# The MLP's second product in seven products of quarters instead of eight, in a two-layer convolution-and-attention kernel

## The chip, the cores and the metric

The kernel runs on one core of one Trainium2 chip. The metric is device time in microseconds (us), from the start of the program to its end. A core has five engines that run side by side[...]: PE (TensorE, matrix products; its weight loads are listed apart as PEld), DVE (VectorE), ACT (ScalarE), POOL (GpSimd) and SP (here only a queue of transfers). SBUF is the on-chip memory; PSUM is the small memory that TensorE writes its products to, in banks of 128 x 512 fp32.

## What is computed

All numbers are fp32. The input is x of 16 images, each 256 channels by 1024 positions. Layer 0 is an attention with 4 heads of 64; layer 1 is group norm, attention with 8 heads of 32, group norm and an MLP of 256, 1024 and 256 channels, each with a residual. Cut to what matters here:

```python
def layer1(x):
    x = x + attention(group_norm(x, gn1_w, gn1_b), qkv_w, proj_w, proj_b, phys_bias)
    h = group_norm(x, gn2_w, gn2_b)
    h = einsum('oc,bchw->bohw', mlp_w1, h) + mlp_b1      # 256 -> 1024
    h = gelu(h, approximate=False)
    h = einsum('oc,bchw->bohw', mlp_w2, h) + mlp_b2      # 1024 -> 256
    return x + h
```

The change concerns the second of the two MLP products, `mlp_w2` times the hidden activations.

## The kernel before

**Tiles.** Channels lie on the 128 partitions. 256 channels are two chunks (CC = 2), 1024 positions are two halves of TB = 512 (NT = 2) or eight blocks of 128 keys (SB = 8), and the 1024 hidden channels are HC = 8 chunks. An fp32 product is issued as two matmul instructions. `product` (L278) splits a product into column strips of width `cols[0]`: 32 during the attentions, 128 between them. So one 128x128 product is 8 matmul instructions during an attention and 2 outside.

**Order.** The order is written out by hand, and each engine takes its instructions in order. For each image b (L904):
1. `attention_a` (layer 0), 32 units of scores, exponentials and weighted sums. Its denominators are summed from the `es_a` tiles.
2. 16 `hidden` pieces (L806) of the *previous* image: product with w1 into PSUM, gelu by ACT into 16 tiles `g`. Between them the rest of layer 0's normalising, projecting and group norm is issued, by `Later.tick`, after so many steps.
3. Half of the layer-1 projections (L927).
4. `attention_b` (layer 1), 16 units, called u0 to u15 below: 4 items (a half of the positions and a chunk of heads), each with 4 steps kb = 0, 2, 4, 6. `fill` (L933 to L955) puts pieces of other work behind single units: the rest of this image's projections in u0 to u3, then the *previous* image's MLP outputs (`reduce`, L820; called o1 to o8) and the *next* image's layer-0 projections (P).

Before the change u4 to u15 hold, in the middle images: o1, o2, P, o3, o4, P, o5, o6, P, o7, o8, P, where a P is 2 or 3 pieces. Image 0 has neither outputs nor P there; the last image has o1 to o4 in u7, u9, u11 and u13, o5 to o8 after its attention, and its own MLP alone at the end.

**One unit of `attention_b`.** TensorE: scores of this unit (L470), the weighted sum of the unit before (L528), at the end of an item the denominator (L552), then the pieces. Scores use bank 0 and bank 1 and three `wide` tiles (L234) of PSUM. There are three `wide` tiles, taken in turn, least recently used first; a piece behind the unit takes the next one. ACT: four exponentials `e_b` (L485), a copy of the first weighted sum of an item. DVE: two adds of `e_b` into `es_b` (L507), the weighted sum added out of PSUM (L541, it frees bank 0 for the next unit), two more `es_b` adds, at some units `scale` (L577, the division by the denominator), and then the piece's own work. Four of the eight `e` tiles are used by a unit.

**Denominators.** `den_copy` (L315) copies the sums by ACT into tile `d`; a transfer spreads them, DVE takes reciprocals, POOL adds both into the range check's totals `dsum` and `isum` (L304, L305), and transfers spread the result into tile `full`, which `scale` reads. In image 0 (items 2 and 3) and the last image (item 3) the last step's `e_b` tiles are not added by DVE but summed by extra denominator matmuls (`spared` and `apart`, L491, L549).

**The output pieces.** For a half of positions t, a chunk of output channels co and a quarter of positions, `reduce` sums eight products of 256 columns and DVE adds bias and residual in one instruction:

```python
for hc in range(HC):
    product(ps, k["w2"][:, hc, co * P : (co + 1) * P],
            gs[t, hc][:, half * n : (half + 1) * n], start=(hc == 0), stop=(hc == HC - 1))
y = xb[:, co, t * TB + half * n : t * TB + (half + 1) * n]
nc.vector.scalar_tensor_tensor(y, ps, k["m2b"][:, co : co + 1], y, ALU.add, ALU.add)
```

**Start.** POOL issues three loads of `wp`, makes the identity `ident` and then issues eight loads of small vectors (L120). `turn` (L876) turns the bias rows `brow` by `ident`; ACT needs the result to empty the first projections. The weights w1 and w2 are loaded by SP (L149).

Of the kernel before, what the change touches and what calls it, by code (L numbers as in the profile page):

```python
# [14 lines left out]
P = 128  # L15
# [39 lines left out]
def kernel(  # L55
# [35 lines left out]
    brow = const.tile([3 * HEADS0 // 2, P], F32, name="brow")  # L91
    for t in (1, 0, 2):
        if t == 0:
            bp = b_proj.rearrange("(g i t d) -> t g i d", i=2, t=3, d=D0)
            for u in range(3):
                nc.scalar.dma_start(
                    brow[u * 2 : (u + 1) * 2].rearrange("g (i d) -> g i d", d=D0), bp[u]
                )
        for cc in range(CC):
            (nc.gpsimd if cc else nc.scalar).dma_start(  # L100
                wp[:, cc, t],
                w_proj[cc * P : (cc + 1) * P, :].rearrange(
                    "p (h t d) -> p t h d", t=3, d=D0
                )[:, t],
            )


# [3 lines left out]
    ident = const.tile([P, P], F32, name="ident")  # L111
    make_identity(nc, ident)
    mhalf = const.tile([P, CC], F32, name="mhalf")
    nc.gpsimd.memset(mhalf, -0.5)
    ones = const.tile([P, D0], F32, name="ones")
# [27 lines left out]
    w2 = load_mat(mlp_w2T, "w2")  # L143


    def load_rest():
# [5 lines left out]
    gind = const.tile([P, P // GSZ], F32, name="gind")  # L152
    nc.vector.tensor_reduce(
        gind, ident.rearrange("p (g j) -> p g j", j=GSZ), AX.X, ALU.add
    )
    gavg = const.tile([P, P // GSZ, GSZ], F32, name="gavg")
    nc.vector.tensor_scalar(
        gavg,
        gind.unsqueeze(2).to_broadcast([P, P // GSZ, GSZ]),
        1.0 / GSZ,  # L160
        None,
        ALU.mult,
    )
    gavg = gavg.rearrange("p g j -> p (g j)")
# [13 lines left out]
    with ExitStack() as first:  # L178
        first_pass(
            first, tc, x, out,  # L180
            dict(
                wp=wp, bqk=bqk, pb=pb, bo=bo, g1w=g1w, g1b=g1b, g2w=g2w,
                g2b=g2b, pjb=pjb, m1b=m1b, m2b=m2b, wo=wo, wq=wq, wpj=wpj, w1=w1,
                w2=w2, ident=ident, gavg=gavg, mhalf=mhalf, ones=ones, eones=eones,
                bvo=bvo, brow=brow, load_rest=load_rest, exp_bias=exp_bias,
                in_range=in_range,
            ),
        )

    good = nc.values_load(in_range[0:1, 0:1], min_val=0, max_val=1)  # L190
    with tc.If(good == 0):
        with ExitStack() as again:
# [5 lines left out]
                    w2=w2, ident=ident, gavg=gavg, mhalf=mhalf, b_proj=b_proj,  # L198
# [4 lines left out]
def first_pass(ctx, tc, x, out, k):  # L203
# [89 lines left out]
    def denominators(key, d, n, waits, then):  # L293
# [3 lines left out]
        full = work.tile([P, CC * TB], F32, tag="full", name=f"rd_{key}", bufs=1)[:, :n]  # L297
# [16 lines left out]

    def den_copy(key, den):  # L315
        d = work.tile([P, TB], F32, tag="d", name=f"d_{key}", bufs=1)
        nc.scalar.copy(d, den)
        return d
# [5 lines left out]
    def attention_a(b, qT, kT, v, project):  # L324
# [58 lines left out]
        def normalise(t):  # L383
            half = TB // 2
            den = wide(f"den_{key}_{t}")[:, 0, :]
            for c in range(CC):
                for g in range(2):
                    for h in range(2):
# [3 lines left out]
                            k["ones"][:, :32],  # L392
# [3 lines left out]
                        )  # L396
            denominators(
                f"{key}_{t}", den_copy(f"{key}_{t}", den), CC * TB,
# [47 lines left out]
    def attention_b(b, qT, kT, v, project):  # L446
# [44 lines left out]
        spared, apart = {0: (2, 3), B - 1: (3,)}.get(b, ()), {}  # L491

        def add(i, kb, es, block):
            if kb == 0 and block == 0:
# [4 lines left out]
                return  # L501
            if i in spared and kb == SB - 2:
                apart[i] = es
                return
# [40 lines left out]
        def normalise(i, r, last):  # L545
# [3 lines left out]
            parts = sums[i] + apart.get(i, [])  # L549
            for m in range(0, len(parts), G // 2):  # L550
                for g in range(G):
                    nc.tensor.matmul(  # L552
                        den[g * D : (g + 1) * D, :],
                        k["eones"][:, c * G + g],
                        parts[m + g // 2][:, g % 2, :],
                        start=(m == 0),
                        stop=(m + G // 2 == len(parts)),
                    )
            if at_end:

                full = work.tile([P, CC * TB], F32, tag="full", name="rd_end", bufs=1)
                nc.vector.reciprocal(full[:, :TB], den)
                scale(i, r, last, full[:, :TB])
                for tot, what in ((dsum, den), (isum, full[:, :TB])):
# [5 lines left out]
                f"{key}_{i}", den_copy(f"{key}_{i}", den), TB,  # L570
# [231 lines left out]

    def mlp(b, xb, hn):
        gs = {}

        def hidden(t, hc):  # L806
# [11 lines left out]
            gs[t, hc] = g  # L818

        def reduce(t, co, half):  # L820
            n = TB // 2
            ps = wide(f"m2_{b}_{t}_{co}_{half}")[:, 0, :n]
            for hc in range(HC):
                product(
                    ps,
                    k["w2"][:, hc, co * P : (co + 1) * P],
                    gs[t, hc][:, half * n : (half + 1) * n],
                    start=(hc == 0),
                    stop=(hc == HC - 1),
                )  # L830
            y = xb[:, co, t * TB + half * n : t * TB + (half + 1) * n]
            nc.vector.scalar_tensor_tensor(
                y, ps, k["m2b"][:, co : co + 1], y, ALU.add, ALU.add
            )

            each = b == B - 1 and (t, co) == (NT - 1, CC - 1)
            if half or each:
                sl = slice(t * TB + (half * n if each else 0), t * TB + (half + 1) * n)
                nc.sync.dma_start(out[b, co * P : (co + 1) * P, sl], xb[:, co, sl])
# [3 lines left out]
            [  # L843
                lambda t=t, co=co, half=half: reduce(t, co, half)
                for t in range(NT) for co in range(CC) for half in range(2)
            ],
# [23 lines left out]
    nothing = work.tile([P, TB], F32, tag="d", name="nothing", bufs=1)  # L870
    nc.vector.memset(nothing, 0.0)
    keep_warm(nothing, 3)
    xs = {0: load_x(0)}
    k["load_rest"]()
    ps, n = bank("bqk", 0), k["brow"].shape[0]
    turn = nc.tensor.transpose(ps[:, :n], k["brow"], k["ident"][:n, :n])  # L876
# [8 lines left out]
    k["exp_bias"]()  # L885

# [17 lines left out]
    for b in range(B):  # L904
# [32 lines left out]
        if b == B - 1:  # L937

            now, end = outputs[:4], outputs[4:]
        if not first:  # L940

            fill = {m: [piece] for m, piece in enumerate(own[:5:2] + own[1::2] + own[6:])}
            fill.update({len(own) + 2 * m: [piece] for m, piece in enumerate(now)})
# [4 lines left out]
        if first:  # L948
            fill[at - 1] = fill[at - 1] + first[:1]
            fill[last + 1] = first[-1:]  # L950
            pairs = [first[1:4], first[4:7], first[7:9], first[9:-1]]
            for m, pair in enumerate(pairs):
                rest.insert(3 * m + 2, pair)
# [20 lines left out]
    for j, (what, most) in enumerate(((dsum, DEN_MAX), (isum, 1.0 / DEN_MIN))):  # L974
        top = small.tile([P, 1], F32, tag="top", name=f"top_{j}")
        nc.vector.tensor_reduce(top, what, AX.X, ALU.add)
        nc.vector.tensor_scalar(ok[:, j : j + 1], top, most, None, ALU.is_le)
    both = small.tile([P, 1], F32, name="both", bufs=1)
    nc.vector.tensor_mul(both, ok[:, 0:1], ok[:, 1:2])
    row = bank("ok_row", 0)  # L980
    nc.tensor.transpose(row[0:1, :P], both, k["ident"])
    least = small.tile([P, 1], F32, name="least", bufs=1)
    nc.vector.tensor_reduce(least[0:1], row[0:1, :P], AX.X, ALU.min)
    nc.vector.tensor_copy(k["in_range"][0:1], least[0:1])


def general_pass(ctx, tc, x, out, k):
# [19 lines left out]
    )  # L1007
    pbs = small.tile([P, HEADS1], F32, name="pbs", bufs=1)
# [8 lines left out]
    def attention(key, H, D, qA, kA, vA, scale, bias, resT):  # L1017
        nb = H // qA.shape[1]
        per = P // D
        for t in range(NT):  # L1020
            tb = slice(t * TB, (t + 1) * TB)
            for h in range(H):
# [17 lines left out]
                for j in range(QT):  # L1040
                    nc.tensor.transpose(
                        row[0:1, j * P : (j + 1) * P], nm[:, j : j + 1], k["ident"]
# [133 lines left out]
    with tc.For_i(0, B, 1) as b:  # L1176
# [38 lines left out]
        for t in range(NT):  # L1215
# [14 lines left out]
            out_proj("gm2", k["w2"], HC, lambda kc: g[:, kc, :], k["m2b"], xb, t, None)  # L1230
# [40 lines left out]
```

## Time and profile before

| what | value |
|---|---|
| median of 3 runs | 3769.32 us (3769.05 to 3769.46) |
| the profiled execution, its own time | 3769.52 us |
| its span | 3767.7 us |
| granted TensorE clock | 1.00 throughout |
| DVE and ACT busy | 59% and 54% of the span |
| `hidden` matmuls, L809 | 1024 x 128x512, 452.8 us |
| emptying of output pieces, L832 | 128 x 128x256, mean 481 ns |
| `es_b` adds, L507 | 884 x 128x1024, mean 1219 ns |
| weighted sums added out of PSUM, L541 | 192 x 128x512, mean 682 ns |
| bias and residual out of PSUM, L617 | 128 x 128x512, mean 746 and 750 ns |
| POOL adds of 128x16, L304 and L305 | 190, median 220 ns |

A row of a group names line, engine, operation, what is written from what, the shape and the count; then busy time, mean duration of one, and the idle time before. A row of the timeline gives start, duration, engine, line, operation and, in brackets, how long its engine was idle before it and what ended that. TensorE's matmuls are pipelined, so the distance of two starts says more than a duration. PE's busy share of 100% is of this kind too.

### The profile page before, as it was taken

The page shows a single profiled execution, that of the slowest core. Times are in us where ns is not written, and L with a number is a line of the kernel's source. Part 1 is how long each engine was busy: PE and PEld are TensorE (multiplying, and loading weights), DVE is VectorE, ACT ScalarE, POOL GpSimd, SP SyncE. Part 2 cuts the span into 40 slices and gives each one's busy share as a digit, 9 for nine tenths or more (in the row PEclk, how much of TensorE's full clock was granted, in tenths as well). Part 3 has the DMA queues.
Part 4 walks back from the last instruction along what each step waited for, and adds up shares of the span by engine and source line. Part 5 has one row for each costly group of instructions (what it writes and reads, how often), then busy time and mean ns, then how long its engine had stood idle before and what let it go on. Part 6 is the DMA issues. An engine that isn't in the chain of part 4 may idle for free.

```text
span 3767.7 us, 87484 instructions
## 1 busy us (share of the span) xinstructions
PE 3755.1 (100%) x38692; PEld 1484.6 (39%) x38692; DVE 2217.2 (59%) x2753; ACT 2035.1 (54%) x2624; POOL 78.2 (2%) x245
## 2 busy tenths in 40 slices
PE   9999999999999999999999999999999999999999
PEld 4334343343433434334343333333333433333335
DVE  4664656646566565665656656565565655646572
ACT  4655546555465554555556455554555556555462
POOL 1000000000000000000000000000000000000000
PEclk9999999999999999999999999999999999999999
DMA  2000000000001000010000000010010100000000
GB/s 85 13 13 13 30 13 16 27 13 30 12 16 33 7 30 12 19 30 8 30 13 22 27 10 28 11 33 16 13 30 7 33 16 13 30 7 22 15 11 23
DMA packets 62352, 78.30 MB, mean 21 GB/s; under 512 B 34990, under 2 KB 36782, under 8 KB 61966
## 3 DMA queue, kind: packets, MB, share of 16 engines
q1 hardware_dynamic: 59820, 71.85, 6.4%
q8 instruction: 304, 4.98, 0.6%
q14 instruction: 82, 0.67, 0.1%
q10 hardware_dynamic: 1746, 0.40, 0.1%
q0 software_dynamic: 400, 0.41, 0.0%
HBM read 54.28 MB, written 17.56 MB: 19 GB/s over the span
## 4 chain that ended last, share of the span: by engine, by line
PE 97%; DVE 1%; issue 1%; ACT 1%; DMA 0%; SPq 0%; DVEq 0%; ACTq 0%
PE s_b L470 13%; PE acc_b L528 12%; PE m L809 12%; PE m L281 12%; PE s_a L338 12%; PE acc_a L359 11%; PE qk_b L281 6%; PE qk_a L281 6%; PE v_b L281 3%; PE o L281 3%; PE v_a L281 3%; PE j L281 3%; PE den_b L552 2%; PE den_a L390 1%; DVE es_a L371 0%
## 5 line engine op out<-in xcount | busy, mean ns | idle before, releaser
L485 ACT ACTIVATE e_b<-s_b 128x1024 f32<-128x1024 f32 (+1 forms) x1280 | 982.7, 864 | 469.8 <-PE s_b L470 469.7
L507 DVE TENSOR_TENSOR es_b<-es_b,e_b 128x1024 f32<-128x1024 f32 x756 | 885.4, 1219 | 339.4 <-ACT e_b L485 339.3
L346 ACT ACTIVATE e_a<-s_a 128x1024 f32<-128x1024 f32 x512 | 521.4, 1025 | 359.7 <-PE s_a L338 349.3
L470 PE MATMUL s_b<-q,k 32*64 32x512 f32 x8192 | 535.5, 601 | 3.1 <-DVE res_b L541 2.4
L338 PE MATMUL s_a<-q,k 64*64 64x512 f32 x4096 | 532.6, 593 | 1.1
L359 PE MATMUL acc_a<-e_a,v 64*64 64x512 f32 x4096 | 528.5, 589 | 0.0
L371 DVE TENSOR_TENSOR es_a<-es_a,e_a 128x1024 f32<-128x1024 f32 x384 | 469.1, 1222 | 85.8 <-ACT e_a L346 73.8
L528 PE MATMUL acc_b<-e_b,v 128*32 128x512 f32 x4096 | 492.1, 598 | 0.0
L281 PE MATMUL m<-g,w 128*32 128x256 f32 (+1 forms) x7616 | 464.3, 379 | 0.0
L809 PE MATMUL m<-gn_h,w 128*128 128x512 f32 x1024 | 452.8, 596 | 0.0
L817 ACT ACTIVATE g<-m,m1b 128x512 f32<-128x512 f32 x256 | 176.0, 687 | 355.9 <-PE m L809 355.9
L281 PEld LDWEIGHTS m<-g,w 128*32 128x32 f32 (+1 forms) x7616 | 277.5, 112 | 215.3 <-issue 41.3
L470 PEld LDWEIGHTS s_b<-q,k 32*64 32x64 f32 x8192 | 174.2, 130 | 287.4 <-issue 146.8
L809 PEld LDWEIGHTS m<-gn_h,w 128*128 128x128 f32 x1024 | 191.0, 190 | 235.5 <-issue 235.2
L359 PEld LDWEIGHTS acc_a<-e_a,v 64*64 64x64 f32 x4096 | 161.9, 133 | 277.5 <-issue 237.2
L338 PEld LDWEIGHTS s_a<-q,k 64*64 64x64 f32 x4096 | 152.6, 133 | 278.1 <-issue 211.7
L541 DVE TENSOR_TENSOR res_b<-res_b,acc_b 128x512 f32<-128x512 f32 x192 | 131.0, 682 | 200.5 <-PE acc_b L528 200.5
L528 PEld LDWEIGHTS acc_b<-e_b,v 128*32 128x32 f32 x4096 | 108.5, 109 | 351.6 <-ACT e_b L485 194.7
L281 PE MATMUL qk_b<-gn_g,wq 128*32 128x512 f32 (+1 forms) x1280 | 234.1, 592 | 0.0
L281 PE MATMUL qk_a<-x,wp 128*32 128x512 f32 (+1 forms) x1856 | 231.1, 592 | 0.5 <-ACT k L722 0.5
L743 DVE TENSOR_TENSOR v<-v_b,eones 128x512 f32<-128x512 f32 x64 | 43.9, 686 | 291.2 <-PE v_b L281 291.2
L507 DVE TENSOR_TENSOR es_b<-e_b,e_b 128x1024 f32<-128x1024 f32 x128 | 150.6, 1217 | 0.0
(124 smaller groups left out, 2087.5 us busy)
## 6 DMA issues: line engine op xcount, KB each, us to landing
rd_a<-row_a SPq DMA_DIRECT2D x64, 256.0 KB
rd_b<-row_b SPq DMA_DIRECT2D x252, 64.0 KB
out_dram<-x SPq DMA_DIRECT2D x63, 256.0 KB
x<-in_x_dram SPq DMA_DIRECT2D x30, 512.0 KB
w<-in_L_conv_mlp_w_dram SPq DMA_DIRECT2D x2, 1024.0 KB
x<-in_x_dram SPq DMA_DIRECT2D x4, 256.0 KB
sp_b<-d_b SPq DMA_DIRECT2D x63, 8.0 KB
row_b<-inv_b SPq DMA_DIRECT2D x63, 8.0 KB
```

The lines of the kernel that those rows point to most:

```text
L281: nc.tensor.matmul(o[sl], w[:, sl], r, **flags)
L338: nc.tensor.matmul(s[h : h + HALF, g, :], kT[g * D : (g + 1) * D, c, kb * P + h : kb * P + h + HALF], qT[g * D : (g + 1) * D, c, t * TB : ...
L346: nc.scalar.activation(e, s, AF.Exp, scale=float(D) ** -0.5)
L359: nc.tensor.matmul(accs[i][h][g * D : (g + 1) * D, :], v[h * HALF : (h + 1) * HALF, kb, c * 2 + g], e[h * HALF : (h + 1) * HALF, g, :], st ...
L371: nc.vector.tensor_add(sums[i], held[i] if kb == 1 else sums[i], e)
L470: nc.tensor.matmul(outs[g][h : h + HALF, :], kT[g * D : (g + 1) * D, c, k0 : k0 + HALF], qT[g * D : (g + 1) * D, c, t * TB : (t + 1) * TB] ...
L485: nc.scalar.activation(to, s, AF.Exp, scale=float(D) ** -0.5)
L507: ins = nc.vector.tensor_add(d, es[n] if kb == 0 else d, es[2 * block + n])
L528: nc.tensor.matmul(acc[g * D : (g + 1) * D, :], v[:, kb + m, c * G + g], es[2 * m + g // 2][:, g % 2, :], start=(m == 0), stop=(m == 1),)
L541: nc.vector.tensor_add(r, r, acc)
L809: nc.tensor.matmul(ps, k["w1"][:, cc, hc * P : (hc + 1) * P], hn[0][:, cc, t * TB : (t + 1) * TB], start=(cc == 0), stop=(cc == CC - 1),)
L817: nc.scalar.activation(g, ps, AF.Gelu, bias=k["m1b"][:, hc : hc + 1])
```

## The change

The second MLP product is seen as a 2 x 2 block product: the weights in quarters A (output chunk by half of the hidden channels), the activations in quarters B (half of the hidden channels by half of the positions). Strassen's scheme forms it from seven products instead of eight; five of them take a sum or difference of two quarters of A, and likewise of B.

- The weights' sums are made once, by POOL, after four loads of quarters.
- The activations' sums are made per image in place, in tiles `g`: four instructions of 128x512 per sum. POOL makes them, for the last image DVE. Two differences are issued among the `hidden` pieces (after the 13th and the 16th), a sum each after products 2, 3 and 4.
- An output piece (o1 to o7) is now one product of 4 chunks and 512 columns. DVE adds or subtracts it into one or two quarters of the output; the first five pieces have two, the last two have one.
- u4 to u15 of the middle images hold o1, P, o2, o3, P, o4, P, o5, P, o6, P, o7, each P two pieces. The last image has o1 to o3 in u7, u10 and u13, the other four after its attention.
- To make room in SBUF: `d` is dropped (`attention_b` copies into `full`, `attention_a` into the tile of `k1`); `brow`, `ident` and `gind` borrow a tile `e` at the start, and with them two of the three loads of `wp` and the identity are issued after the small vectors and the first x; `spared` and `apart` are gone. The range check at the end takes a matmul with `ones` in place of a transpose.

```diff
+    w2s = const.tile([P, 7, HID // P // 2, P], F32, name="w2s")
...
+    for n, q in ((2, (0, 0)), (3, (1, 1)), (4, (0, 1)), (1, (1, 0))):
+        weights.append((w2s[:, n], quarter(*q)))
+    def sum_quarters():
+        q11, q22 = w2s[:, 2], w2s[:, 3]
+        nc.gpsimd.tensor_sub(w2s[:, 5], w2s[:, 1], q11)
+        nc.gpsimd.tensor_add(w2s[:, 1], w2s[:, 1], q22)
+        nc.gpsimd.tensor_sub(w2s[:, 6], w2s[:, 4], q22)
+        nc.gpsimd.tensor_add(w2s[:, 4], w2s[:, 4], q11)
+        nc.gpsimd.tensor_add(w2s[:, 0], q11, q22)
...
-    def denominators(key, d, n, waits, then):
+    def denominators(key, den, d, full, waits, then):
+        nc.scalar.copy(d, den)
...
-            if i in spared and kb == SB - 2:
-                apart[i] = es
-                return
...
     def mlp(b, xb, hn):
+        n4 = HC // 2
         gs = {}
+        add_to = nc.gpsimd if b < B - 1 else nc.vector
...
-            gs[t, hc] = g
+            gs[hc // n4, t, hc % n4] = g
+            if (t, hc) == (1, n4):
+                combine((1, 0), (0, 0), False)
+            if (t, hc) == (1, HC - 1):
+                combine((0, 1), (1, 1), False)
+
+        def combine(to, what, plus):
+            for i in range(n4):
+                d = gs[(*to, i)]
+                ins = (add_to.tensor_add if plus else add_to.tensor_sub)(
+                    d, d, gs[(*what, i)]
+                )
+                tc.keep_in_program_order(ins)
+
+        products = [
+            (2, (0, 0), [(1, 0, True, True), (1, 1, False, False)], ((0, 0), (1, 1))),
+            (5, (1, 1), [(0, 1, True, True), (0, 0, False, False)], None),
+            (3, (0, 1), [(0, 1, True, False), (1, 1, True, True)], ((0, 1), (0, 0))),
+            (4, (1, 0), [(0, 0, True, True), (1, 0, True, False)], ((1, 0), (0, 0))),
+            (1, (0, 0), [(0, 0, True, False), (1, 1, True, False)], None),
+            (6, (0, 1), [(1, 1, True, False)], None),
+            (7, (1, 0), [(0, 0, True, False)], None),
+        ]
+        missing = {(0, 0): 4, (0, 1): 2, (1, 0): 2, (1, 1): 4}
+
+        def reduce(number, right, outs, then):
+            ps = wide(f"m2_{b}_{number}")[:, 0, :]
+            for i in range(n4):
+                product(
+                    ps, k["w2s"][:, number - 1, i], gs[(*right, i)],
+                    start=(i == 0), stop=(i == n4 - 1),
+                )
+            for co, t, plus, bias in outs:
+                missing[co, t] -= 1
+                num = 2 if b == B - 1 and number == 7 else 1
+                for u in range(num):
+                    n = TB // num
+                    sl = slice(t * TB + u * n, t * TB + (u + 1) * n)
+                    y, p = xb[:, co, sl], ps[:, u * n : (u + 1) * n]
+                    if bias:
+                        nc.vector.scalar_tensor_tensor(
+                            y, p, k["m2b"][:, co : co + 1], y, ALU.add, ALU.add
+                        )
+                    elif plus:
+                        nc.vector.tensor_add(y, y, p)
+                    else:
+                        nc.vector.tensor_sub(y, y, p)
+                    if not missing[co, t]:
+                        nc.sync.dma_start(out[b, co * P : (co + 1) * P, sl], y)
+            if then:
+                combine(*then, True)
...
     xs = {0: load_x(0)}
+    brow, ident = k["at_start"](
+        work.tile([P, 2, TB], F32, tag="e", name="borrowed", bufs=8)
+    )
     k["load_rest"]()
...
     k["exp_bias"]()
+    k["sum_quarters"]()
...
-            now, end = outputs[:4], outputs[4:]
+            now, end = outputs[:3], outputs[3:]
...
-            fill.update({len(own) + 2 * m: [piece] for m, piece in enumerate(now)})
+            fill.update({len(own) + 3 * m: [piece] for m, piece in enumerate(now)})
...
-            pairs = [first[1:4], first[4:7], first[7:9], first[9:-1]]
-            for m, pair in enumerate(pairs):
-                rest.insert(3 * m + 2, pair)
+            for m, at_most in enumerate((1, 4, 6, 8, 10)):
+                rest.insert(at_most, first[2 * m + 1 : 2 * m + 3])
```

In `products` each row is: number, which quarter of B, the outputs it is added to (co, t, plus or minus, with bias or not), and the sum made in place after it.

## The prediction

> **What bounds the kernel now.** I read the page's busy line and chain of waits first, then the timeline of one image's second attention by engine (PE, DVE, PEld), then POOL.
>
> ```profile
> PE 3755.1 (100%) x38692; PEld 1484.6 (39%) x38692; DVE 2217.2 (59%) x2753; ACT 2035.1 (54%) x2624; POOL 78.2 (2%) x245
> ...
> PE 97%; DVE 1%; issue 1%; ACT 1%; DMA 0%; SPq 0%; DVEq 0%; ACTq 0%
> ...
> L281 PE MATMUL m<-g,w 128*32 128x256 f32 (+1 forms) x7616 | 464.3, 379 | 0.0
> ```
>
> TensorE is never idle and is 97% of the chain; the product to be shortened is 464.3 us of it. So any TensorE time removed or lost counts in full. But a "busy" PE also hides short waits, as its timeline shows:
>
> ```profile
> 2732.64 3.64 PE L281 MATMUL m<-g,w 128*32 128x256 f32 x64
> 2736.20 2.40 PE L470 MATMUL s_b<-q,k 32*64 32x512 f32 x32
> 2738.53 1.92 PE L528 MATMUL acc_b<-e_b,v 128*32 128x512 f32 x16
> 2740.27 3.64 PE L281 MATMUL m<-g,w 128*32 128x256 f32 x64
> 2743.84 1.97 PE L470 MATMUL s_b<-q,k 32*64 32x512 f32 x32
> 2745.74 1.92 PE L528 MATMUL acc_b<-e_b,v 128*32 128x512 f32 x16
> ```
> ```profile
> 2734.11 2.35 DVE L507 TENSOR_TENSOR es_b<-es_b,e_b 128x1024 f32<-128x1024 f32 x2
> 2736.38 0.68 DVE L577 TENSOR_TENSOR res_b<-res_b,rd_b 128x512 f32<-128x512 f32 x1
> 2736.98 0.48 DVE L832 SCALAR_TENSOR_TENSOR x<-m,m2b,x 128x256 f32<-128x256 f32 x1
> ```
> ```profile
> 2737.51 0.21 PEld L470 LDWEIGHTS s_b<-q,k 32*64 32x64 f32 x8 [0.24 <-DVE x L832]
> ```
>
> An output piece takes 3.57 (2732.64 to 2736.20). The scores after it took 2.33 from start to start (2736.20 to 2738.53), the next ones 1.90 (2743.84 to 2745.74): 0.43 lost. The last line names why: the last eight loads of the scores wait for DVE's L832. Every unit takes three `wide` PSUM tiles and the piece at its end a fourth, so the last tile of the next unit's scores is the one that the output piece wrote, and DVE must have emptied it. Two more cases in the last image (scores at 3633.34 and 3658.49) took 1.99 and 2.22, with L832 ending 0.91 and 1.14 after their start; above it ended 1.26 after. Losses 0.09, 0.32, 0.43 for 0.91, 1.14, 1.26 are one line: **loss = (end of the emptying, after the start of the next scores) - 0.82 us.** In an undisturbed unit DVE starts 0.14 after the scores do (2743.97 against 2743.84) and needs 0.48: nothing is lost.
>
> ```profile
> 198.98 1.10 POOL L304 TENSOR_TENSOR dsum<-dsum,sp_b 128x16 f32<-128x16 f32 x1 [17.01 <-DMA sp_b<-d_b]
> ```
> ```profile
> 198.78 4.66 DVE L507 TENSOR_TENSOR es_b<-es_b,e_b 128x1024 f32<-128x1024 f32 x4 [2.01 <-ACT e_b L485]
> ```
>
> A POOL add of 16 columns has a median of 0.22 us; this one, issued inside a DVE add that runs from 198.78 to about 200.0, ended at 200.08. POOL waited for the running DVE add, then got in before DVE's next.
>
> **What the Trainium skill says.** GPSIMD Engine Reference, section 3.1: a two-input fp32 add of 2048 columns took 4497 ns. No row here has such a width. From that and the 0.22 us at 16 columns I estimate 0.22 + 496 x 2.1 ns = 1.25 us for 512 (proportionally it would be 1.12). SBUF — State Buffer, section Who interferes with whom: a DVE instruction with two SBUF inputs contends with a GpSimd one that reads SBUF, the second to issue waiting; one with at most one SBUF input, outside the 2-port modes, does not. The first half agrees with 1.10 against 0.22; no run here shows the second. So `es_b` adds (both inputs in SBUF) will collide with the new sums, and adds out of PSUM should not.
>
> **The change, part by part.** In us; u4 is unit 4 of the 16 in the second attention.
>
> *TensorE.* Seven pieces of 32 matmul instructions at 512 columns replace eight of 64 at 256. `qk_a` shows the new shape: 48 in 5.27, so 32 in 3.5, the same as now. One piece per image goes: -3.57 in images 1 to 14, and the two waits of 0.43 go (now o5 in u10 and o8 in u14, both behind a `scale`): -0.86. That is -4.43 per image, the whole gain. The image period is 233.0 (`hidden` pieces start at 2613.34 and 2846.34).
>
> *Emptying the products.* Five of seven products are now added twice, over 512 columns. From L617, a bias add is 0.75 and the next instruction starts 0.66 after it; from L541, an add out of PSUM is 0.68 with 0.60 to the next. Each pair ends 0.14 + 0.66 + 0.68 = 1.48 after the scores start: 1.48 - 0.82 = 0.66 lost. By place:
> - o1 in u4, o4 in u9: 0.66 each. o3 in u7: 0.14 + 0.60 + 0.75, 0.67.
> - o2 in u6, where `scale` is due: DVE ends its `es_b` adds 7.38 into the unit (2703.28 against 2695.90), `scale` takes 0.60, the unit 7.21; so it starts at 0.77, ends at 2.11: 1.29 lost.
> - o5 in u11: two plain adds, 0.60, and 0.18 more from the contention below.
> - o6 in u13: one add, ends at 0.82, nothing. o7 in u15 is followed by no scores.
> Sum 4.06. The other units, u5, u8, u10, u12 and u14, hold projection pieces, which ACT empties.
>
> *Sums on POOL, images 0 to 14.* Eight subtractions lie in the hidden stage, behind the `rstd_g` power in POOL's queue (2634.83, after 10 of 16 hidden pieces; the first sum is emitted after 13), where DVE has only one-input work: nothing. Twelve additions, four each after o1, o3 and o4, start with the next unit. Alternating with `es_b` adds at 1.25 they delay the adds of u5 by some 2.9, to 9.7 after its start, while the unit, stretched by 0.66, takes 7.87 and the next `es_b` start 2.24 into u6: no loss. In u8 two of four `es_b` adds are absent. In u10, with `scale`, DVE ends at 10.25, and u11 begins its adds 0.15 to 0.18 late: the 0.18 above. The summed inputs are wanted in u11, u13 and u15, over 30 us later. Queued behind them on POOL are only `dsum` and `isum`, which nothing waits for, until `rstd_h` in the next stage. Bounds: 0 if they never collide; 3 per image if POOL keeps the port for its four adds in a row.
>
> Images 1 to 14: 14 x (-4.43 + 4.06) = **-5.2**.
>
> *No more `apart`.* Image 0, items 2 and 3, and image 15, item 3, lose 16 denominator matmuls each (194.42 to 196.25, 1.83) and get four `es_b` adds (4 x 1.14) on DVE. There units without pieces run at DVE's pace, 5 us against TensorE's 3.64. For item 2, the result add that the next unit's bank 0 waits for comes some 1.1 later, most of which the missing 1.83 pays: -0.7. For item 3, -1.8. Image 0: **-2.5** (from -4 to +5, where all eight adds would count). Image 15: one piece less among its units (u7, u10, u13 instead of u7, u9, u11, u13), but pairs of adds at DVE's pace and sums beside them; at the end the 3.36 reciprocal sets the pace, some 0.5 earlier: **-0.5** (-3 to +4).
>
> *The tail.* Seven pieces of 3.45 instead of eight (128 matmuls from 3733.39 to 3761): -3.45. Image 15's 20 sums run on DVE at 0.60, beside pieces of 3.45. The last product is emptied in halves, +0.35: **-3.1**.
>
> *The start.* On POOL `wp` for q and v and the identity now stand behind eight small loads of 0.74: 5.9 later. q's weights then land about 13.5 instead of 7.6; TensorE can do k's four pieces until 14.2, if they come first: **+1.5** (0 to 4). SP issues four quarters instead of one `w2`; they are wanted 250 us later. The five weight sums make POOL wait for them, with `dsum` at 64 us behind. `full` taking over from `d`, and `k1` in the first attention, have their old readers gone a unit or a stage before; nothing.
>
> Sum: -5.2 - 2.5 - 0.5 - 3.1 + 1.5 = -9.8 on a span of 3767.7, with 1.8 around it (run 3769.5): **3759.7**; the median shown is 0.2 below that run, so **3759.5**.
>
> **Rivals.**
> *Faster: the tile is free in time.* If the loss line does not hold beyond 1.26, the 3.57 is kept. For: all four losses seen are 0.43 or less. Against: three points on one line, and the load that names L832. Without any new loss: 3769.3 - 14 x 4.43 - 4.6 = 3703; with half of it 3731.
> *Slower: the POOL sums hold up the emptying itself.* Place: after o1, o3 and o4 the first sum is released by the same last matmul as DVE's pair. If an add with one SBUF input also waits for POOL, each pair ends one sum later: 1.25 x 42 = +52, so 3812; two sums, 3864. It decides from 0.42 per place (17.5 / 42), which takes the time over 3777. For: a TENSOR_TENSOR is the operation that made POOL wait above. Against: the skill's exception.
> *The change doesn't do what it says*, for instance TensorE waiting for late sums: 30 us of room against 5 us of work excludes it.
>
> **How the numbers follow.** Forecast 0.56 (3744 to 3776: the bounds of contention, image 0 and the start), faster rival 0.22, slower one 0.22. The measurement cannot tell changes within 0.2%, 7.5 us. Half of the forecast, and somewhat more, lies below 3761.8, most of the rest within 7.5 of before: faster 0.57, same 0.21, slower 0.22. The range cuts a tenth off either side: 3718 to 3792.
>
> **What would show it.** Right: period 232.6; L281 m of 3320 matmuls; `s_b` after o1, o3, o4 and o5 taking about 2.56, after o2 3.2, with loads waiting for DVE at the output adds, some 50 us over the trace; POOL adds of 128x512 at 1.25. Wrong: `s_b` at 1.90 there (faster rival), or output adds starting 1 us or more after the scores (slower one); a period below 231 or above 234.

## The result, and the profile after

| | before | after |
|---|---|---|
| median of runs beside each other | 3769.73 | 3781.56 |
| span of the profiled execution | 3767.7 | 3780.4 |
| its mean granted TensorE clock | 1.000 | 0.998 |

The ratio is 1.0031, with a 95% interval of 1.002 to 1.0042: the change made the kernel slower by 0.31%, where a fall of 0.27% was forecast. The time lies inside the range given (3718 to 3792), on the other side of the time before. One of the four runs of experiment e6 below was slow (4792.31 us at a granted clock of 0.752, the others at 0.998 or 0.999), and e6's time is the median of the other three.

First the page of the changed kernel: busy time by engine, the shares of the chain that ended last by engine, and the groups that the change touches.

```profile
PE 3751.6 (99%) x34349; PEld 1329.2 (35%) x34349; DVE 2459.8 (65%) x2850; ACT 2036.6 (54%) x2624; POOL 565.4 (15%) x550
...
PE 90%; DVE 4%; issue 3%; DMA 1%; ACT 1%; SPq 0%; POOL 0%; DVEq 0%; ACTq 0%; POOLq 0%
...
L527 DVE TENSOR_TENSOR es_b<-es_b,e_b 128x1024 f32<-128x1024 f32 x768 | 961.5, 1300 | 258.2 <-ACT e_b L512 256.5
...
L497 PE MATMUL s_b<-q,k 32*64 32x512 f32 x8192 | 588.9, 603 | 14.9 <-DVE x L895 6.8
L855 POOL TENSOR_TENSOR g<-g,g 128x512 f32<-128x512 f32 x300 | 458.8, 1553 | 760.4 <-PE m L309 739.7
...
L309 PE MATMUL m<-g,w2s 128*32 128x512 f32 (+1 forms) x3320 | 404.2, 592 | 0.0
```

The product has shrunk from 464.3 to 404.2 us of TensorE, so 60 us were really saved. TensorE is still 99% busy, but its share of the chain has fallen from 97% to 90% and VectorE's has risen from 1% to 4%: TensorE now waits, and most of that waiting is booked as busy time of the scores (`s_b`, 588.9 in all).

The span was then cut at five points found in the timeline: the first scores of image 0, the first `hidden` piece of images 0 and 14, the first of image 15, and the end. "Stage of image 15" is everything between the last two of these pieces.

| part of the span | predicted | before | after | measured |
|---|---|---|---|---|
| start, to the first scores | +1.5 | 28.22 | 34.08 | +5.9 |
| image 0, to its `hidden` | -2.5 | 255.19 | 253.02 | -2.2 |
| images 1 to 14, period | -5.2 | 233.00 | 233.45 | +6.4 |
| stage of image 15 | -0.5 | 160.60 | 166.03 | +5.4 |
| tail | -3.1 | 61.82 | 58.95 | -2.9 |
| sum | -9.8 | | | +12.6 |

Three lines of the table failed: the middle images, the start and the stage of image 15. They are shown in this order, from the timeline of the changed kernel (columns: start in us, duration in us, engine, line, operation, tiles and shapes, count, and in brackets the idle time before it with what ended it). Middle images first, the product o3 in a middle image:

```profile
2717.08 3.62 PE L309 MATMUL m<-g,w2s 128*32 128x512 f32 x32
...
2717.94 3.44 DVE L527 TENSOR_TENSOR es_b<-es_b,e_b 128x1024 f32<-128x1024 f32 x2
...
2718.30 6.67 POOL L855 TENSOR_TENSOR g<-g,g 128x512 f32<-128x512 f32 x4 [12.92 <-PE m L309]
...
2720.63 1.95 PE L497 MATMUL s_b<-q,k 32*64 32x512 f32 x24
...
2721.30 0.68 DVE L893 TENSOR_TENSOR x<-x,m 128x512 f32<-128x512 f32 x1
...
2721.90 0.74 DVE L889 SCALAR_TENSOR_TENSOR x<-m,m2b,x 128x512 f32<-128x512 f32 x1
...
2722.78 1.09 PE L497 MATMUL s_b<-q,k 32*64 32x512 f32 x8 [0.21 <-DVE x L889]
2723.80 0.16 PEld L548 LDWEIGHTS acc_b<-e_b,v 128*32 128x32 f32 x8 [0.81 <-ACT e_b L512]
```

The last eight matmuls of the scores wait for L889, the second add of the product, as predicted. It ends at 2722.64, 2.01 after the scores' start, and from scores to sums it takes 3.17 instead of 1.90: 1.27 lost, where 0.67 was predicted. The reason is POOL's row: its sums start at 2718.30, while the product still runs, because its matmuls release the tiles `g` one after the other. So they meet the `es_b` adds of the *same* unit (3.44 instead of 2.35), and VectorE reaches the product's adds 0.5 later.

The five places account for the period: 0.75, 1.40, 1.27, 0.75 and 0.74 are lost after o1 to o5, 4.91 in all, and 233.00 - 4.43 + 4.91 = 233.48, against 233.45 measured.

The start:

```profile
8.25 1.53 POOL L93 DMA_DIRECT2D wp<-in_L_conv_w_proj_dram  x2
...
10.57 1.12 PE L309 MATMUL qk_a<-x,wp 128*128 128x512 f32 x2
...
15.12 12.12 PE L309 MATMUL qk_a<-x,wp 128*128 128x512 f32 x22 [3.43 <-DMA wp<-in_L_conv_w_proj_dram]
```

POOL issues `wp` for q and v at 8.25, behind eight small loads. TensorE has two pieces of k and half a piece of q to do and then stands for 3.43. That is not the whole cost. From 13.2 to 20.0 the clock granted to TensorE was 0.50. A view of that stretch shows it (PEclk, the third figure from the end, is the granted clock):

```profile
core 0: us, PE busy (x) PEld busy (x) DVE busy (x) ACT busy (x) POOL busy (x), PEclk, DMA share, GB/s
13.20:20.00 6.80, 4.88 (x6) 2.18 (x7) 0.00 (x0) 0.69 (x1) 0.00 (x0) 0.50 1.09 332
```

The 4.9 us of matmuls from 15.12 to 20.0 ran at that clock, so some 2.4 more were lost: with the wait, 5.8 of the 5.9.

The stage of image 15, where no projections lie beside the attention:

```profile
3641.07 6.93 POOL L855 TENSOR_TENSOR g<-g,g 128x512 f32<-128x512 f32 x4 [8.43 <-PE m L309]
...
3641.59 4.06 DVE L527 TENSOR_TENSOR es_b<-es_b,e_b 128x1024 f32<-128x1024 f32 x2
...
3643.40 1.95 PE L497 MATMUL s_b<-q,k 32*64 32x512 f32 x24
...
3646.23 0.67 DVE L895 TENSOR_TENSOR x<-x,m 128x512 f32<-128x512 f32 x1
...
3647.05 1.09 PE L497 MATMUL s_b<-q,k 32*64 32x512 f32 x8 [1.70 <-DVE x L895]
```

Here VectorE is busy back to back, so the two `es_b` adds that POOL stretches from 2.35 to 4.06 are passed on whole, and TensorE idles 1.70. A second wait, 1.81 at 3691.53, ends with the result add that frees bank 0, behind another stretched pair. Here too the clock counts. After each of the two waits it was 0.50 for 3.41 us. In e3, an experiment below that changes only the start, the stage has waits of 1.71 and 1.82 but no such spell. The same view of the stage, first of the changed kernel, then of e3:

```profile
3555.39:3721.42 166.03, 161.31 (x1236) 56.14 (x1233) 117.35 (x142) 83.29 (x113) 33.09 (x32) 0.98 0.05 14
```
```profile
3552.90:3716.14 163.24, 158.05 (x1236) 55.69 (x1233) 117.36 (x142) 83.30 (x113) 33.10 (x32) 1.00 0.05 14
```

So 2.8 of the 5.4 are the two spells, and 2.6 are left.

### The profile page after: what moved, and what is told of

Its sections match the earlier page's. It is cut to its first block, busy times and chain, and to the rows that moved or that the text cites. A ratio compares the mean times of both kernels' runs of the same rounds, so it can differ in the third digit from the quotient of the medians.

```text
span 3780.4 us, 79539 instructions
## 1 busy us (share of the span) xinstructions
PE 3751.6 (99%) x34349; PEld 1329.2 (35%) x34349; DVE 2459.8 (65%) x2850; ACT 2036.6 (54%) x2624; POOL 565.4 (15%) x550
## 4 chain that ended last, share of the span: by engine, by line
PE 90%; DVE 4%; issue 3%; DMA 1%; ACT 1%; SPq 0%; POOL 0%; DVEq 0%; ACTq 0%; POOLq 0%
PE s_b L497 12%; PE m L836 12%; PE s_a L363 12%; PE acc_b L548 11%; PE acc_a L384 11%; PE m L309 7%; PE qk_b L309 6%; PE qk_a L309 5%; PE v_b L309 3%; PE o L309 3%; PE v_a L309 3%; PE j L309 3%; DVE es_b L527 2%; PE den_b L570 1%; PE den_a L415 1%
## 5 line engine op out<-in xcount | busy, mean ns | idle before, releaser
L527 DVE TENSOR_TENSOR es_b<-es_b,e_b 128x1024 f32<-128x1024 f32 x768 | 961.5, 1300 | 258.2 <-ACT e_b L512 256.5
L497 PE MATMUL s_b<-q,k 32*64 32x512 f32 x8192 | 588.9, 603 | 14.9 <-DVE x L895 6.8
L855 POOL TENSOR_TENSOR g<-g,g 128x512 f32<-128x512 f32 x300 | 458.8, 1553 | 760.4 <-PE m L309 739.7
L309 PE MATMUL m<-g,w2s 128*32 128x512 f32 (+1 forms) x3320 | 404.2, 592 | 0.0
L309 PEld LDWEIGHTS m<-g,w2s 128*32 128x32 f32 (+1 forms) x3320 | 122.2, 112 | 261.5 <-issue 246.6
```

The costliest lines, as they stand in the source:

```text
L309: nc.tensor.matmul(o[sl], w[:, sl], r, **flags)
L497: nc.tensor.matmul(outs[g][h : h + HALF, :], kT[g * D : (g + 1) * D, c, k0 : k0 + HALF], qT[g * D : (g + 1) * D, c, t * TB : (t + 1) * TB] ...
L527: ins = nc.vector.tensor_add(d, es[n] if kb == 0 else d, es[2 * block + n])
L855: ins = (add_to.tensor_add if plus else add_to.tensor_sub)(d, d, gs[(*what, i)])
```

## The experiments

Theory A: a product's PSUM tile is emptied too late, because VectorE first ends the unit's `es_b` adds and then needs two adds of 512 columns; POOL's sums make that worse only where they meet `es_b`. Rival B: POOL's sums are the loss. Rival C: VectorE's load is. The kernel before, run beside them, had medians of 3769.6 to 3770.0. All edits are to the changed kernel.

**e1_single_add.** Each product is added into its first output only (the counts in `missing` are set to match).

```diff
-            for co, t, plus, bias in outs:
+            for co, t, plus, bias in outs[:1]:
```

> Leaves out the second of the two adds of each of the products o1 to o5 (five of twelve adds per image), so part of the output's sum is missing; products, POOL sums, loads and order stay. Theory A (TensorE waits because the product's PSUM tile is emptied by two adds of 512 columns, 1.4 to 2.1 us after the next scores start, and every us past 0.74 is lost): with one add the emptying ends at about 0.14 + 0.68 = 0.82, after o2 (behind the scale) at about 1.45. So the losses of 0.75, 1.40, 1.27, 0.74, 0.74 fall to about 0.1, 0.7, 0.6 (o3 keeps what the POOL sums do to the adds before it), 0.1, 0.1: from 4.9 to 1.6 per image, 14 x 3.3 = 46 us, some 4 more in image 15's adds: about 3732, period 230.2. Rival B (the POOL sums beside the adds are the loss): the sums are still there, so the time stays within 10 us of 3781. Rival C (VectorE's total load): five adds of 0.67 less per image is under 2% of VectorE's busy time; a change of under 10 us.

Measured: 3737.56, ratio to before 0.9911 (0.9896 to 0.9927), 44.0 below the changed kernel; period 230.39. The timeline of TensorE in this run, after o1, o2 and o3:

```profile
2667.01 2.03 PE L497 MATMUL s_b<-q,k 32*64 32x512 f32 x32
2668.97 1.92 PE L548 MATMUL acc_b<-e_b,v 128*32 128x512 f32 x16
...
2681.45 2.68 PE L497 MATMUL s_b<-q,k 32*64 32x512 f32 x32
2684.06 1.92 PE L548 MATMUL acc_b<-e_b,v 128*32 128x512 f32 x16
...
2689.34 2.48 PE L497 MATMUL s_b<-q,k 32*64 32x512 f32 x32
2691.76 1.92 PE L548 MATMUL acc_b<-e_b,v 128*32 128x512 f32 x16
```

From start to start 1.96, 2.61 and 2.42: losses of 0.06, 0.71 and 0.52, against 0.75, 1.40 and 1.27. After o4 the loss is 0.06, after o5 0.42 where 0.1 was expected; why is not known. POOL's sums are unchanged here and `es_b` still has a mean of 1298 ns, so B falls as the main cause: one add less behind the `es_b` adds is worth 43 us in the middle images. C is not yet excluded: the five adds left out are 3.35 us of VectorE per image, about as much as the period fell. It falls in e6, where VectorE has more to do and the kernel is faster.

**e2_no_sums.** The in-place sums are left out.

```diff
-            for i in range(n4):
+            for i in range(0):
                 d = gs[(*to, i)]
```

> Leaves out the twenty in-place sums of activations of each image (on POOL in images 0 to 14, on VectorE in image 15), so that products 2 to 7 get other inputs; everything else stays. Theory A: only what these sums do to the es_b adds beside them goes: 0.6 per image after o3 (loss 1.27 to about 0.67), 14 x 0.6 = 8 us; in image 15's stage the two waits of 1.70 and 1.81 shrink, 3 to 5 us; at the end nearly nothing. About 3768, period 232.8. Rival B (the sums are what makes the change slower): the losses after o1, o3 and o4 all fall to near nothing, period about 230, time about 3735 or less.

Measured: 3767.08, ratio 0.9992 (0.9983 to 1.0), 14.5 below the changed kernel. The period is 232.92, so the sums cost 0.53 in each of 14 images, 7.4 in all. All of it is at o3, where the loss falls from 1.27 to 0.75; the other four places lose what they lost with the sums. The stage of image 15 falls from 166.0 to 158.6, by 7.5: 4.7 when compared with e3's stage without half-clock spells (163.24), and 2.8 for the two spells, which are gone together with the waits. So the whole rise of image 15, and 2.0 more, goes with POOL's sums. They are a real cost, but not the main one.

**e3_start** and **e7_start.** In e3 the loads of `wp` for q and v go directly behind those for k. In e7 the eight small loads go behind them instead:

```diff
         t = const.tile([P, n], F32, name=name)
-        nc.gpsimd.dma_start(t, v.rearrange("(c p) -> p c", p=P))
+        vectors.append((t, v.rearrange("(c p) -> p c", p=P)))
...
         make_identity(nc, ident)
+        for v, src in vectors:
+            nc.gpsimd.dma_start(v, src)
```

> The loads of the first attention's projection weights for q and v are issued directly after those for k, ahead of the small vectors, the identity and the load of the first image, as in the kernel before; nothing else changes. Theory A (5.9 us at the start are POOL's late issue of wp for q, for which TensorE waits 3.4 with only k's pieces to do): the first scores start 4 to 6 us earlier, at 28 to 30, and the whole time falls by that: about 3776.5. Rival (the start is set by the identity and the transposed bias, or by the later loads): no change, or slower by up to 2 us, since the identity and the biases' loads now come later.

> Only the loads of the eight small vectors move, behind wp for q and v and the identity in POOL's queue; ScalarE's queue keeps the bias rows ahead of its wp loads for q and v, which e3 had put behind them (TensorE then waited 2.69 for those rows). Theory A (the start costs what POOL's late wp costs): q's weights come before k's pieces end, first scores at 28 to 29.5 instead of 34.1, time about 3776. Rival (loads share one bandwidth, so the start is set by bytes): first scores stay at 31 or later.

e3: 3779.14, ratio 1.0023 (1.0014 to 1.0032); first scores at 31.72, less than expected, because the bias rows now stood behind `wp` in ScalarE's queue. e7: 3774.63, ratio 1.0012 (1.0006 to 1.0019), 6.9 below the changed kernel; first scores at 27.74. Its timeline:

```profile
2.44 1.50 POOL L93 DMA_DIRECT2D wp<-in_L_conv_w_proj_dram  x2
```
```profile
10.09 10.81 PE L313 MATMUL qk_a<-x,wp 128*128 128x512 f32 x24
...
27.74 1.95 PE L367 MATMUL s_a<-q,k 64*64 64x512 f32 x16
```

With `wp` issued at 2.44 the 24 matmuls run through without a wait, and the granted clock is 1.00 up to the first scores. So the start's +5.9, the wait and the spell of half clock with it, came from the place in POOL's queue.

**e4_order.** Only the order of the pieces changes: a product that is added twice has a projection piece behind it in the same unit.

```diff
-            for m, at_most in enumerate((1, 4, 6, 8, 10)):
-                rest.insert(at_most, first[2 * m + 1 : 2 * m + 3])
+            p = first[1:-1]
+            rest = [
+                [now[0], p[0]], [p[1]], [now[1], p[2]], [now[2], p[3]],
+                [p[4]], [p[5]], [now[3], p[6]], [now[4], p[7]],
+                [p[8]], [now[5]], [p[9]], [now[6]],
+            ]
```

> Only the order of the pieces in images 1 to 14 changes: in units 4 to 15 each product that is added twice is followed by a projection piece in the same unit (3.5 us on TensorE), units with one projection piece stand where pairs stood; number of pieces, sums and adds are the same, nothing is left out. Theory A (the loss is the emptying ending too late for the next scores' tile): VectorE is through with the unit's es_b adds before the piece that follows the product ends, so both adds end before the next scores start; the losses of 0.75, 1.40, 1.27, 0.74 and 0.74 go to 0 to 0.2 each: about 4.4 x 14 = 60 us, time about 3720, period 229.1. Rival B (contention of POOL sums with es_b adds slows the stage): the sums still run beside es_b adds, so at most 10 us are gained. Rival C (VectorE's load in the stage): no change.

Measured: 3776.67, ratio 1.0015 (1.0008 to 1.0022), only 4.9 below the changed kernel: a miss by 55. (A projection piece is also half as long as I wrote, 1.8 us.) The timeline shows why. After o1 theory A holds:

```profile
2695.76 0.75 DVE L889 SCALAR_TENSOR_TENSOR x<-m,m2b,x 128x512 f32<-128x512 f32 x1 [1.33 <-PE m L309]
...
2696.43 0.68 DVE L895 TENSOR_TENSOR x<-x,m 128x512 f32<-128x512 f32 x1
...
2697.34 1.97 PE L497 MATMUL s_b<-q,k 32*64 32x512 f32 x32
...
2699.24 0.16 PEld L548 LDWEIGHTS acc_b<-e_b,v 128*32 128x32 f32 x8 [0.81 <-ACT e_b L512]
```

Both adds end before the scores start, and from start to start it takes 1.90: nothing lost. After o2 and o5 nothing is lost either. But o4, now in a unit with `es_b` adds and a `scale`, met POOL's sums:

```profile
2738.36 7.39 POOL L855 TENSOR_TENSOR g<-g,g 128x512 f32<-128x512 f32 x4 [2.89 <-PE m L309]
...
2738.68 4.27 DVE L527 TENSOR_TENSOR es_b<-es_b,e_b 128x1024 f32<-128x1024 f32 x2
...
2742.47 1.11 PE L497 MATMUL s_b<-q,k 32*64 32x512 f32 x16
...
2742.87 1.76 DVE L595 TENSOR_TENSOR res_b<-res_b,rd_b 128x512 f32<-128x512 f32 x1
...
2744.55 0.74 DVE L889 SCALAR_TENSOR_TENSOR x<-m,m2b,x 128x512 f32<-128x512 f32 x1
2745.21 0.67 DVE L893 TENSOR_TENSOR x<-x,m 128x512 f32<-128x512 f32 x1
...
2746.03 1.12 PE L497 MATMUL s_b<-q,k 32*64 32x512 f32 x16 [2.44 <-DVE x L893]
```

The `es_b` pair takes 1.92 longer and the `scale` 1.08 longer, so the emptying starts 3.0 late. With two pieces in the unit the product's tile is wanted one step earlier too, by the second half of the scores, which wait 2.44. In all, 2.70 are lost after o4, and after o3, in the same way, 1.08.

The mean period of 233.15 hides a second thing. In eight of the 14 middle images it is 232.37 to 232.40. In the other six it is 233.71 to 235.38, and in each of these, beside the wait after o4, the granted clock was 0.50 for 3.41 us (in one 6.83). The 20 runs of e4 agree: the fastest, 3768.73, had a mean clock of 0.998, the slowest, 3783.12, one of 0.993. So without these spells the order alone is worth 1.07 per image.

So either theory A is incomplete, with a second limit behind the first, or the shorter units are the trouble. The next three runs separate these.

**e5_order_no_sums.** The edits of e4 and e2 together.

> The order of e4 without the in-place sums of activations (all twenty per image left out, so products 2 to 7 get other inputs). In e4 the losses after o1, o2 and o5 went, but o4's unit lost 2.9 on the scores and 1.5 on the product after them, while four POOL sums of 7.39 in all ran beside es_b adds (2 in 4.27 instead of 2.35) and the scale (1.76 instead of 0.68). Theory A with contention as second limit: without the sums both go, period about 228.6 (233.0 less 4.43), so 14 x 4.2 = 58 us below the run without sums in the old order: about 3709. Rival D (e4's gain is eaten because units with half a projection piece, 5.5 us, are too short for VectorE's 4.66 of es_b adds): the waits stay without the sums, time within 15 of 3767.

Measured: 3706.84, ratio 0.983 (0.9815 to 0.9845), period 228.62. The scores' group of this run:

```profile
L497 PE MATMUL s_b<-q,k 32*64 32x512 f32 x8192 | 527.6, 601 | 3.9 <-DVE res_b L561 2.6
```

`s_b` has fallen from 588.9 to 527.6 us, and the period is that of before less the 4.43 of the prediction's first step (228.57). The short units do no harm, so rival D falls. It also accounts for e4: with 1.08 and 2.70 lost, 228.60 becomes 232.38, the period of e4's images at full clock.

**e8_dve_only** and **e6_order_dve.** The twelve sums after o1, o3 and o4 on VectorE, in the old order and in that of e4, for images 0 to 13.

```diff
+            eng = nc.vector if plus and b < B - 2 else add_to
             for i in range(n4):
                 d = gs[(*to, i)]
-                ins = (add_to.tensor_add if plus else add_to.tensor_sub)(
+                ins = (eng.tensor_add if plus else eng.tensor_sub)(
```

> The changed kernel's order, with the twelve additions on VectorE instead of POOL in images 0 to 13; nothing left out. Theory A: the losses after o1, o2, o4 and o5 stay (two adds still end 1.4 to 2.1 after the next scores start), o3's falls by 0.6; the four sums behind o1, o3 and o4 end 2.4 later than the pair, pushing the next unit's es_b adds by about 1.7, which may cost o2 up to 1 more: 3775 to 3795. Rival B (POOL contention is the loss): about 3735 or less.

> The order of e4, and the twelve additions after o1, o3 and o4 on VectorE instead of POOL in images 0 to 13 (0.60 each, behind the product's own adds in VectorE's program); nothing left out. Theory A with contention: VectorE stands idle 2.5 to 3.2 behind the adds of o1 and o3 in e4, so 2.4 of sums fit there, behind o4 they push the next es_b adds by about 1.5, which the product in that unit covers; waits for the output adds go; period 228.6 to 229.2, images 1 to 14 about 60 below the changed kernel: about 3722 (3715 to 3735). Rival C (VectorE's load is the limit): 7.2 us more on VectorE per image make it slower than e4: 3777 or more.

e8: 3773.67, ratio 1.0009 (1.0 to 1.0017), period 232.95: as good as without sums (232.92), a little better than expected. e6: 3714.62, ratio 0.985 (0.9832 to 0.9868), period 228.73, nothing left out. The timeline around o4 in e6:

```profile
2691.37 2.36 DVE L527 TENSOR_TENSOR es_b<-es_b,e_b 128x1024 f32<-128x1024 f32 x2
...
2693.64 0.69 DVE L595 TENSOR_TENSOR res_b<-res_b,rd_b 128x512 f32<-128x512 f32 x1
...
2694.25 0.75 DVE L890 SCALAR_TENSOR_TENSOR x<-m,m2b,x 128x512 f32<-128x512 f32 x1
2694.91 0.68 DVE L894 TENSOR_TENSOR x<-x,m 128x512 f32<-128x512 f32 x1
...
2695.17 1.97 PE L497 MATMUL s_b<-q,k 32*64 32x512 f32 x32
...
2695.50 2.49 DVE L856 TENSOR_TENSOR g<-g,g 128x512 f32<-128x512 f32 x4
```

The same chain is undisturbed, ends 0.42 after the scores start (2695.59), and the sums follow in 2.49, behind what TensorE waits for. So the engine with the larger load does the sums at almost no cost (228.73 against 228.62 without any), and the idle one was the costly place. Rival C falls: with the twelve sums VectorE is busy for 2499.2 us of the run, against 2468.8 in e4, and the kernel is faster; e8, with 2501.9, has the same work and still loses 4.4 per image at the five places.

Set side by side, the four periods tell it best:

| sums on | old order | order of e4 |
|---|---|---|
| POOL | 233.45 | 233.15 |
| VectorE | 232.95 | 228.73 |

Either change alone is worth 0.3 to 0.5 per image, both 4.72. At full clock the order alone would be worth 1.07, which leaves the picture as it is: each change removes one of two limits, and the gain comes when both are gone.

**e9_both.** The edits of e6 and e7.

> The order and the VectorE additions of e6 together with the loads of e7; nothing left out. Theory A: the parts are in different places of the trace and add up: 3715.2 of e6 less 7.0 (e7 against the changed kernel): about 3708 to 3711, 1.6% below the kernel before. Rival (what is gained at the start is lost again later, as waits that only the start's offset had hidden): 3715.

Measured: 3706.95, ratio 0.9835 (0.9822 to 0.9849): 1.65% faster than the kernel before, and nothing left out. That is 1 us below the range expected; counted from e6's 3714.6 the sum of the parts is 3707.7, so they add up. In its stage of image 15 (164.3), where the sums of image 14 are still on POOL, some 6 us are left by comparison with e5 (158.6), one spell of half clock among them; no run tried to get them.

## Why the prediction was wrong

Forecast and measurement are 22.4 us apart, from -9.8 to +12.6: 11.6 in the middle images, 5.9 in the stage of image 15, 4.4 at the start and 0.5 in the rest. The middle images alone, with their two terms, take the sum to +1.8; no single term would have turned the sign.

*TensorE, -4.43 per image:* right; e5 and e6 show it almost whole (periods of 228.62 and 228.73, against 233.00 before).

*Emptying the products:* the mechanism was right, and all five places lose as named: 0.75, 1.40, 1.27, 0.75 and 0.74, the same in all 14 images, against 0.66, 1.29, 0.67, 0.66 and 0.78. Two terms were mis-sized. The constant of the loss line, 0.82 from ends of 0.91 to 1.26, is 0.74 at ends of 1.48 to 2.14 (1.48 - 0.75, 2.14 - 1.40, 2.01 - 1.27): some 0.08 at each place. At o5 this is hidden, because 0.18 had been allowed for contention and the loss is 0.74 with the sums and without them (e2). So 0.3 per image is left, and no run explains it. The other term is o3, next.

*Sums on POOL:* the step that failed is "Twelve additions, four each after o1, o3 and o4, start with the next unit." At o1 and o3 they start inside the product, 1.2 us after its first matmul. At o3 they meet `es_b` adds that stand ahead of the emptying, and that cost 0.52 (1.27 against 0.75 without sums, e2), 7.3 over 14 images. At o1 the `es_b` adds beside them end in time, since VectorE then waits 1.33 for the product. At o4 they start with the next unit, as I had written, because `isum` stands ahead of them on POOL; there, as worked out, they were hidden. Together the two terms make +0.84 per image, 11.8 over 14 images, which turned -5.2 into +6.4 (measured by the period). The sum of the middle images was a small difference of two large terms, 4.43 and 4.06, so 20% of one was enough to change its sign.

*Image 15, -0.5 (-3 to +4):* this failed, at +5.4 it left even its bounds. "sums beside them" got no number of its own; they measured 4.7, since nothing hides them in a stage that runs at VectorE's pace, and the two spells of half clock after their waits 2.8 more. Without them the stage is 2.0 shorter than before (e2). Without the spells the rise would have been 2.6, inside the bounds.

*The start, +1.5:* failed. "TensorE can do k's four pieces until 14.2, if they come first" left the condition open: two come first, and the third piece is q's. TensorE waited 3.43, and the half clock beside the wait, for which the prediction has no term anywhere, cost some 2.4 more. The total was 5.9.

*Image 0 and the tail:* right, -2.2 and -2.9 against -2.5 and -3.1.

*The 1.25 us for a POOL add of 512 columns,* worked out from the GPSIMD Engine Reference, section 3.1: undisturbed ones took 1.26 and 1.27. (0.22 + 496 x 2.1 ns is in fact 1.26.) The mean of 1553 ns includes the waiting for VectorE.

*Rivals.* The faster one is excluded: the line keeps rising beyond 1.26, one us lost for each us later. The slower one had the sign but not the mechanism. The timeline of the changed kernel around o1, with POOL's sums running:

```profile
2694.59 4.73 POOL L855 TENSOR_TENSOR g<-g,g 128x512 f32<-128x512 f32 x3 [39.32 <-PE m L309]
...
2696.92 2.72 PE L497 MATMUL s_b<-q,k 32*64 32x512 f32 x32
2697.06 0.75 DVE L889 SCALAR_TENSOR_TENSOR x<-m,m2b,x 128x512 f32<-128x512 f32 x1 [1.33 <-PE m L309]
...
2697.72 0.68 DVE L895 TENSOR_TENSOR x<-x,m 128x512 f32<-128x512 f32 x1
```

The adds out of PSUM start 0.14 after the scores and take 0.75 and 0.68, as without POOL's sums (e2). That agrees with the Trainium skill (SBUF — State Buffer, Who interferes with whom): an add with one input in SBUF is not held up, one with two is. It is the adds *ahead* of the emptying in VectorE's queue, `es_b` and `scale`, that POOL delays.

## What to carry to other kernels

When a change makes one engine's tiles larger or has them read more often, look up who wants the tile next and what stands ahead of the reader in its queue; if the tile is wanted at once, put other work of the producer between. Here that paid only once the reader was not held up ahead of the tile as well (e4 against e6). Work put on an idle GpSimd was not free for VectorE: ask when its *first* input is released, not its last, and which two-input adds run then; behind the critical reads on VectorE itself it may cost less. And where a sum is the difference of two terms of nearly the same size, a fifth of either decides its sign, so the stages at the edges, first and last image, need as much care as the loop.

## What the runs showed of the hardware that was not expected

**Half clock beside waits.** In the traces of this case the clock granted to TensorE is 1.00 or 0.50, and 0.50 comes in spells of 3.41 or 6.83 us. Leaving aside the end of each run, after TensorE's last matmul, there are 23 such spells in eleven traces. Each lies beside a wait of TensorE of 1.70 us or more, overlapping it or starting within 1.9 us of its end, and none lies elsewhere; the next longest waits after the first matmul are of 1.01 and had none. But only 23 of the 37 waits of 1.70 or more had a spell: all eight at the start (2.69 to 4.95), six of 14 in e4's middle images (2.44), nine of 15 in the stage of image 15 (1.70 to 2.58). What decides was not tried. So here a wait of 1.7 us could cost some 1.4 more than its length.

**POOL beside one-tile work.** POOL's subtractions in the `hidden` stage also held up VectorE work that reads a single tile from SBUF. The timeline of the changed kernel:

```profile
2643.74 4.95 POOL L855 TENSOR_TENSOR g<-g,g 128x512 f32<-128x512 f32 x4
2643.81 1.21 DVE L707 TENSOR_TENSOR ga_g<-rstd_g,g1w 128x2 f32<-128x2 f32 x1 [0.82 <-POOL rstd_g L705]
...
2647.52 4.75 DVE L717 TENSOR_SCALAR gn_g<-x,ga_g,gc_g 128x512 f32<-128x512 f32 x4
```

`ga_g`, a product of two SBUF tiles of two columns, took 1.21 us instead of the 0.16 of the kernel before, about one POOL subtraction (4.95 for four) more; with two SBUF inputs that is as the section of the Trainium skill named above has it (SBUF — State Buffer, Who interferes with whom). The four `gn_g`, one tile and two columns of scalars each, took 4.75 instead of 1.91. That section lets an operation with at most one SBUF input, outside the 2-port modes, pass; these did not. It also lists this kind of operation (TENSOR_SCALAR) among those that can enter such a mode, so `gn_g` need not contradict it. Whether it ran in one was not tried. That the scalar columns count as a second input is less likely: L889 above also reads a tile and a column from SBUF, and took its 0.75. It cost nothing here: `gn_g` ended at 2652.27, and the projection that reads it started at 2653.04.
